# Two graph layers, fused: the hand-made order of VectorE, ScalarE and GpSimd is dropped, that of TensorE and the transfers is kept

## The chip, the cores and the metric

One NeuronCore of one Trainium2 chip runs the whole program. The metric is the device time of one execution in microseconds. For the kernel before it is 2702.02 us, the median of three runs (2701.94 to 2702.38).

## What is computed

The input `x` is 128 graphs of 128 nodes with 256 features, and `adj` is a 128x128 adjacency matrix of 0 and 1 for each graph. Everything is float32. Two layers follow each other:

```python
# layer 0: two graph attentions, then a feed-forward of 1024 with Relu
h = gat(x, W1, a1); h = gat(h, W2, a2)     # softmax over axis 1 of leaky_relu(Wh1 + Wh2^T), masked by adj
h = layernorm(x + h); x = layernorm(h + relu(h @ w_ff1) @ w_ff2)
# layer 1: 8 heads of 32, values by relation (adj == r), then a feed-forward of 1024 with Gelu
attn = softmax(q k^T / sqrt(32)); out = sum_r (attn * (adj == r)) @ v_r
x = layernorm(x + out @ Wo); x = layernorm(x + gelu(x @ W1) @ W2)
```

## The kernel before

**Tiling.** Four graphs make a group (`G = 4`), so there are 32 groups. A group passes through five stages: `load`, `gat` (both graph attentions and the first normalisation), `ff0` (Relu feed-forward), `att` (heads) and `ff1` (Gelu feed-forward). Several groups are in flight at once, each in another stage. A first part of the program, `graph_layers` (L1073), does the graph attentions of groups 0 to 2 and `ff0` of group 0, prepares the weights, and scans the whole adjacency for values other than 0 and 1; a branch (L1157) then takes one of two versions of the rest. With these inputs it is always `BINARY`; the other, `GENERAL`, is compiled but not run.

**Each stage is a generator.** It issues some instructions and then yields a number. `run` (L958) pops the stage with the smallest time from a heap, lets it issue its next piece, and pushes it back at its time plus the step. So a timetable (`begin`, `steps`, `early`, `period=100` units for one group) decides the order in which all pieces are traced. One group took about 80 us on the chip, so a unit is some 0.8 us.

**From the timetable to queues.** After each piece `run` looks at the instructions just traced. Those of TensorE and SyncE (`kept`, which issues all transfers) enter their engine's queue at the piece's time. Those of the other three engines enter their engine's queue at the piece's time plus a number from the table `lags`, where such a number is given:

```python
        for i in reversed(new):
            lag = 0 if i.engine in kept else None
            if behind.get(i.engine):
                lag = behind[i.engine].pop(0) if len(behind[i.engine]) > 1 else behind[i.engine][0]
            if lag is not None:
                queues.setdefault(i.engine, []).append((round(t + lag, 3), len(queues.get(i.engine, ())), i))
            elif lags is not None and PE in queues:
                after(i, queues[PE][-1][2])
...
    for queue in queues.values():
        queue.sort(key=lambda x: x[:2])
        for (_, _, first), (_, _, i) in zip(queue, queue[1:]):
            after(i, first)
```

Every queue is sorted by time, and each instruction is tied behind the one before it. `after` adds an ordering edge for the compiler's scheduler (`NoSync`: it fixes the order of issue and adds no semaphore). An instruction without a lag is tied only behind the last TensorE instruction that was traced before it. Among what such edges leave open the compiler chooses, with its own simulated run of the program (`schedule_with_timeline_sim=True`, L1207).

**The lag tables.** A table has one line for each piece of a stage. In it `V`, `S` and `G` are VectorE, ScalarE and GpSimd, and the numbers are lags in timetable units for that engine's instructions in that piece, the last number serving for all that follow. `BINARY` has tables for `gat`, `ff0`, `att`, `ff1`, and separate ones for some stages of the first and the last group (L77 to L251). `PREFIX`, the first part's plan, has its own (L280 to L354). `lag_table` (L996) reads them. Most numbers of `BINARY` lie near 100; only differences between them matter, since each engine has its own queue. Some stand out: the first four VectorE statistics of `att`'s last piece have 45.9 to 59.3, the affine of `att`'s second half has 9 and 14.1 on GpSimd.

**The pieces that the prediction speaks of.**
- `feed_forward` (L641) does its products by a scheme with fewer multiplications. `unit` (L651) makes one half of the hidden features in four visits; two units are interleaved by `order=(0, 0, 1, 0, 1, 0, 1, 1)`. Each visit is two `product` calls (L656, matmuls at L658) into two PSUM tiles, `chain` and `side`. Between visits the other engines read partial sums out of the same tiles, and only then may TensorE go on into them: L664 (ScalarE copies `chain`) and L665 (VectorE adds `side`) after the first visit, L669 and L670 (ScalarE copies both) after the second, L674 and L675 (VectorE adds both) after the third, and the activations L679 and L683 (ScalarE) after the fourth. The second product is at L714, and its results are added into `y` by VectorE at L719.
- `normalised` (L571) is statistics on VectorE (L577, L578, L580), a power on GpSimd (L582), one VectorE product (L583) and four scalings on ScalarE (L585). `affine` (L587, L591) is two GpSimd instructions for each two graphs.
- `put` (L593) turns a tile: VectorE transposes 32x32 blocks (L608), SyncE stores it to DRAM (L611), and `get` (L615) reads it back (L617).
- `attention` (L818): query and key (L828 to L834), scores (L849), maxima on VectorE (L853), exponentials on ScalarE (L862), division on GpSimd (L865), turning, the mask on VectorE (L884), the values (L899, L900), the weighted sum (L913), its copy (L917) and the output product (L940, L941).
- `gat_block` (L786): features (L794, copied at L795), scores and softmax (L769 to L783), and weighted sums (L802, copied at L803, and L813).

Of the kernel before, what the change touches and what calls it, by code (L numbers as in the profile page):

```python
# [25 lines left out]
G = 4  # L26
# [19 lines left out]
    lags={},  # L46
# [10 lines left out]
        gat=(  # L57
            3.6, 5.8, 1.7, 17.4, 23.25, 4.55, 12.25, 11.5, 16.85,
        ),
        ff0=(  # L60
            1.45, 19.1, 6.85, 4.85, 5.95, 3.1, 5.95, 0.1, 0.3, 0.5, 0.6, 0.4, 0.3, 0.25, 17.5, 0.2,
            0.3,
        ),
# [10 lines left out]
        (-2, "ff1"): -2, (-1, "load"): -2, (-1, "ff1"): -5, (3, "load"): 24, (-4, "load"): -10,  # L74
        (4, "load"): -7, (5, "load"): -1, (-5, "load"): -6,
    },
    lags={  # L77
        "gat": """
V 15.2 | S 104.7 95
S 102.8 104.1  # L80
V 99.9
|
V 102.7 104.7 105.4 117.1 | S 110.4 110.8 110.6 106 112.8 113.3 111.3 112.7 | G 113.4
S 97.7 98.3 99.6 100.4
V 96.7
|
V 84.8 85.6 88.4 99.3 | S 84.3 87.2 88.1 86.4 96.8 90.8 90.2 98.2 | G 102.7
V 91.7 93 92.1 92.3 93.3 95.1 96.7 97.9 98 98.2 98.4 98.6 | S 102.1 99.8 99.4 97 | G 100.7
""",
        "ff0": """  # L90
V 95.8
|
G 92.7 103.2 97.6 110.4
V 107.9 | S 107.3
S 104.3 104.8
V 102.9 | S 103.6 | G 54.9 67.7
V 103.6 104.5
S 98.8 100.9 | G 48.3 50.9
S 103.9 99.6 100.9 105 102.3 98.5
V 101.1 103.3  # L100
S 104.4 106.1 105.3 105.9 106.7 104.2
|
V 101.6 104.3 | G 106.4 100.5
V 105.4 107 | G 110.3
V 105.3 108.1 108.5 | G 104.5
V 96.3 97.5
V 100.9
V 104.4 105.5 100.6 101.4 101.5 106 106.2 107 106.6 107.1 107.3 108.7 | S 111.8 112.5 114.6 110.7 | G 107.2
""",
        "att": """  # L110
V 100.7
|
V 106.7 105 | S 102.9 114
V 103.9 106.2 107.4 108.2 110.6 117.5 | S 110.9 112.3 112.9 114.7 113.6 116 115.6 116.9 116.9 121.2 117.3 119.6 120.1 120.9 119.5 120.3 | G 110.5 119.3
V 96.6 103
|
V 110.5 112 | G 55.4 67
V 122.1 129.6
V 105.4 105.6 107.4 107.6 111.5 115.5 | S 104.5 107 108.4 107.3 108.7 108.8 109.6 109 109.9 110.5 114.3 113.2 113.6 110.2 112 113.5 115.4 | G 111.2 116.4
V 97  # L120
V 92.1 95.8
|
V 96.8 98.8 | G 9 14.1
V 106.8 108.6
S 119.4
V 105.5
V 45.9 54.2 50.8 59.3 99.3 99.9 99.7 100 100.5 102.8 | S 103.8 104 105.6 104.7 | G 97.4
""",
        "ff1": """
V 87.7  # L130
|
G 96.4 96.4 111.7 103.9
V 94.9 | S 93.9
S 100.6 92.2
V 92.8 | S 93.3 | G 48.2 62.3
V 96.3 103
S 93.3 93.9 | G 43.6 51.8
S 101.5 102.2 96.5 102.9 90.8 104.9
V 98.6 101.8
S 102.4 102.7 102 102.9 99.4 101.4  # L140
|
V 100 107 | G 92.1 106.8
V 99.7 111.4 | G 101
V 94.7 96 99.5 | G 92.2
V 97.3 100.3
V 101.3
V 65.3 67.6 64.2 64.3 66.8 68.5 70.1 72.5 70.2 72.4 74.1 75.6 | S 77.5 80.2 78.3 76.4 | G 70.5
G 34.5 80.5
G 45.7 46.4
""",  # L150
        "ff0 -1": """
V 100.1 | S 97.2
|
G 71.5 75.6 91.9 103.7
V 109.3 | S 106.9
S 104.2 106.8
V 102.4 | S 101.1 | G 68 76.2
V 105.3 101.8
S 95.4 97.11 | G 59 72.5
S 96.8 99 101.8 104.5 101.3 96  # L160
V 100.8 102.3
S 107.5 110.3 110 110.3 104.5 105.8
|
V 99.5 101.1 | G 102 107.7
V 104.2 109.7 | G 112.9
V 109.6 110.6 113.1 | G 107
V 100.1 101.3
V 101.17
V 103.9 105.7 100.99 102.2 102.1 102.6 105.9 107.2 106.1 106.48 107.8 111 | S 105.12 106.3 106.55 106.8 | G 111
""",  # L170
        "att 0": """
V 119.5 111.85 113.2 113.3 114.4 120.5 116.2 114.8 103.4 109.5 120.6 128.2 107.7 119 112.8 | S 142.2
|
V 105.3 103.7 | S 125.3 129.53
V 105.7 111.1 113 113.3 116.2 119.6 | S 125.46 125.69 125.91 126.9 126.6 126.6 126.82 127.28 127.05 129 127.2 128.2 127.5 128.9 128.64 128.87 | G 109.3 111.2
V 102.2 109.9 | S 110.35 118.1
|
V 103 112.3 | G 66.7 80.2
V 101.7 115
V 102.6 105.9 106.2 107.57 109.2 120.2 | S 98.4 101.2 103 100.3 100.9 102.6 106.3 104.6 111.7 104.4 107 113.3 114 107.7 114.3 115.1 116.9 | G 105.5 121.2  # L180
V 95.8
V 97.05 108.1 | S 102.7 120.3
|
V 104.6 115 | G 12.3 13.3
V 99.4 100
S 112
V 101.3
V 43.7 48 44.1 52.4 95.45 96.2 95.8 97.5 98.61 104.5 | S 105 109.5 109.2 108.7 | G 97
""",
        "att -1": """  # L190
V 101.6 | S 108.7
|
V 106.8 95.7 | S 101.3 101.8
V 103.2 105.6 106 106.5 112 115.8 | S 98.6 102.7 101.6 103.7 104.7 107.8 105.8 110.9 107.4 111 111.5 120 113.1 116.2 112.1 113.7 | G 111 115.6
V 99.3 101.74 | S 102.6 106.2
|
V 108.3 110.8 | G 60.1 61.3
V 99.2 102.1
V 90.2 93.7 96.7 103.7 104.7 107.2 | S 84.3 90.9 95.5 90.7 93.8 102.6 104.2 94.9 98.5 104.3 107.4 97.6 105.2 104.5 110.1 106.8 111.4 | G 90.7 96.2
V 85.8  # L200
V 98 89.3 | S 90.1 93
|
V 95.3 110.7 | G 2 6.7
V 89.8 103.6
S 93.9
V 101.8
V 43.19 53 43.6 45.4 97.3 101.93 101.85 102 102.5 103.1 | S 84.8 87.7 94 104.3 | G 92.5
""",
        "ff1 0": """
V 86.9  # L210
|
G 89.9 91.7 101 107.5
V 94.2 | S 94.56
S 90.9 93.8
V 96 | S 95 | G 48.8 53.4
V 95.6 96.2
S 92.3 92.4 | G 51.8 70.9
S 96 90.2 96.2 99.3 98.6 99.8
V 97 99.3
S 100.6 94.6 96.6 107.6 97.6 102.6  # L220
|
V 97.7 106 | G 103.9 100.1
V 103.5 107.5 | G 104.6
V 94 94.8 98.6 | G 94.1
V 96.2 97.2
V 100.1
V 66.5 68 67.5 70 67.8 71.2 70.8 71.4 71.72 72 73.9 76.4 | S 77.48 75.9 78.2 91.5 | G 70
G 39.2 54.7
G 38.6 59.9
""",  # L230
        "ff1 -1": """
V 83 | S 82.9
|
G 64.85 66.7 68.1 68
V 57.9 | S 65.5
S 62.5 62.1
V 48.2 | S 57.5 | G 40.1 53.8
V 48.8 54
S 68.4 77 | G 44.4 56.4
S 61.7 69 76.2 84.3 53.5 56.1  # L240
V 50.8 53.65
S 82.5 85.1 81.8 86.4 82.1 77.2
|
V 44.6 46.9 | G 61 83.5
V 52.7 53.4 | G 83.6
V 33.7 37.4 40.5 | G 64.3
V 37.4 41.6
V 40.6
V 4.1 9.9 7.3 9.6 10.8 15.3 13.43 15.1 18.9 20.3 20.1 23.4 25.6 28.1 27.3 28.4 32.8 32.9 | S 28.5 26.1 31.7 40.8 | G 33.8 58.3
""",  # L250
    },  # L251
)

PREFIX = dict(
# [22 lines left out]
        34, 39.75, 6.05, 33.25, 5.05, 21.05, 9.55, 19.25, 27.55, 11.55, 13.25, 8.55, 3.55, 1.55,  # L277
        4.05, 65.25, 46.05,
    ),
    lags={  # L280
        (0, 0): """
V 2 | S 16.4 3
S 9.2 4.3
|
V -15.1 -13.2 -1.6 -1.2 -0.7 -0.6 1.2 2.6 | S -4.6 -4.6 -4.6 -3.5 -1.9 -1.5 0 -1.5 | G 3 6.9
S -13.8 -11.9 -11.6 -10.3
|
V -14.6 -13.7 -12.8 -12.7 -12.4 -9.6 -9.7 -8.2 | S -22.4 -18.4 -16.6 -15.6 -13.4 -12.4 -9.4 -9.5 | G -22.2 -20.9
V -6.8 -5.6 -4.9 -3.6 -4 -3.2 -2.6 -1.8 -2.2 -1.8 -1.4 0.8 | S 0.5 0.6 3.2 3.3 | G -4.5
""",  # L290
        (0, 1): """
V 17.1 | S 14.6 16.2
S 11.3 12.6
|
V -7 -3.6 0.1 1.5 4.6 5.5 8 9 | S -9 -8 -7.5 -7 -0.2 -2.2 6.8 5.2 | G 11.3 13.8
S -20.8 -19.7 -20.6 -18.7
|
V -61.8 -60.3 -60 -59.7 -59.1 -58.1 -53.9 -46.9 | S -64.8 -64.3 -64.3 -62.8 -56.9 -55 -56.7 -53.6 | G -48.1 -42.3
V -84.5 -84.3 -83 -82.6 -83 -80.8 -81.2 -79.4 -79.3 -78.9 -75.9 -65.9 | S -66.6 -82.5 -61.4 -79.8 | G -75
""",  # L300
        (0, 2): """
V 15.7 | S 4.4 -1
S 3 6.1
|
V -9.2 -8.5 -7 -8 -6.6 -6.3 -3.8 -2.2 | S -13.6 -12.1 -11.5 -10.3 -7.9 -7 -1.8 -6.3 | G -10.5 -1.1
S -19.8 -19.5 -18.7 -18.3
|
V -52.3 -47.6 -46.8 -47.9 -47.2 -46.9 -44 -40.5 | S -57 -53.7 -53.7 -52.7 -44.2 -43.7 -42.8 -44.8 | G -52.7 -46.2
V -55.8 -53 -52.8 -52 -52.4 -50.2 -51.1 -50.8 -50.7 -49.5 -49.2 -44.6 | S -50.3 -33.2 -37.1 -41.5 | G -56.3
""",  # L310
        (1, 0): """
V -11.8 | S -11.8
|
G -35.3 -34.3 -33.4 -32.6
V -35.2 | S -36.1
S -45.8 -44.8
V -42.6 | S -44.7 | G -56.2 -55.6
V -55.4 -54
S -55 -54.5 | G -69.2 -57.6
S -57.4 -58.1 -56.2 -50.1 -55.1 -57.6  # L320
V -75 -73.7
S -87.6 -85.9 -84.1 -83.2 -85.1 -85.1
|
V -119.7 -116.8 | G -126.8 -118.6
V -136.2 -134.6 | G -132.5
V -135.8 -135.7 -135 | G -134.7
V -155.9 -155.1
V -157.4
V -194.8 -191.1 -196.4 -194.2 -195.5 -191 -190.4 -189.1 -189.5 -189 -180.8 -180.6 | S -192.8 -195.1 -193 -182.4 | G -198.9
""",  # L330
        (2, 0): """
V 11.9 13.1 11 13.3 14.7 19.9 15.7 18.2 18.9 19 24.5 21.7
V -53.6 -43.2 -42 -24.2 -47.9 -40.1 -32.2 -32.5 -40
""",
        (3, 0): """
|
V -34.5
S -44
V -69.8
S -77.1  # L340
V -83.5
S -105.3
V -123.1
S -130.4
V -149.7
S -155.3
V -151.6
S -157.7
V -156.4
S -164  # L350
V -212.8
S -264.5
""",
    },  # L354
)

_COLS = {
    "bf1": "L0_gnn_b_ff1", "b1": "L1_gnn_b1", "bq": "L1_gnn_bq", "bk": "L1_gnn_bk",
# [852 lines left out]
```

## Time and profile before

| | |
|---|---|
| median of three runs | 2702.02 us |
| the profiled execution's own time | 2707.46 us |
| its span, first to last instruction | 2705.6 us |
| mean granted TensorE clock | 0.985 |
| busy share of the span | TensorE 98%, VectorE 77%, ScalarE 61%, GpSimd 62% |
| SyncE-issued transfers, share of 16 DMA engines | 52.2% |

PE is TensorE's matmuls, PEld its weight loads, DVE VectorE, ACT ScalarE, POOL GpSimd and SP SyncE. In a row of costliest groups, the text before the bar names line, engine, operation, tiles (out<-in) and shapes with the count; behind it stand the busy time, the mean duration in ns, and the engine's idle time before these instructions with what ended it. In the view of waits a row is who waited, for what, the total us, how many times and the longest. In the timeline a row is start, duration, engine, line and operation, with idle time before it in brackets. In a table of windows each row is a stretch of the span with the busy time of PE, PEld, DVE, ACT and POOL, the granted clock, the DMA share and GB/s.

### The profile page before, as it was taken

The numbers are of one execution on the slowest core, as the hardware profiler recorded it, in microseconds if no ns is written. First come the engines' busy times: TensorE is split into PE (matmuls) and PEld (weight loads), VectorE is DVE, ScalarE is ACT, GpSimd is POOL, SyncE is SP. The second block draws the span as 40 slices with busy tenths as digits, with TensorE's granted clock in tenths as the row PEclk, the third lists the DMA queues.
The fourth block names the chain that finished last, engine by engine and source line by source line (L and its number), as shares of the span: only waits on it lengthen the run. The fifth ranks groups of instructions, "written<-read, shape, count | busy, mean of one in ns | idle before, by whom it ended". The sixth has DMA issues, their size and how long they took to land.

```text
span 2705.6 us, 54054 instructions
## 1 busy us (share of the span) xinstructions
PE 2638.0 (98%) x19686; PEld 2181.8 (81%) x19686; DVE 2090.2 (77%) x3922; ACT 1638.7 (61%) x4957; POOL 1675.0 (62%) x1354
## 2 busy tenths in 40 slices
PE   7789999999999999999999999999999999999997
PEld 5668888888888888888888888888888888888767
DVE  5657887787887788888788888778788778788654
ACT  5346666656666666666666666665666665665543
POOL 2435676667566667666666666666656666766654
PEclk8899999999999999999999999999999999999999
DMA  8125555655655655655655555565554565555310
GB/s 301 33 59 133 114 112 132 139 119 130 128 106 122 149 126 118 131 116 115 140 130 119 133 117 113 133 139 118 131 127 105 125 148 126 115 123 113 77 46 24
DMA packets 1137579, 323.71 MB, mean 120 GB/s; under 512 B 886424, under 2 KB 1106072, under 8 KB 1137176
## 3 DMA queue, kind: packets, MB, share of 16 engines
q1 hardware_dynamic: 1137304, 320.17, 52.2%
q8 instruction: 157, 2.57, 0.4%
q14 instruction: 118, 0.97, 0.1%
HBM read 192.57 MB, written 127.52 MB: 118 GB/s over the span
## 4 chain that ended last, share of the span: by engine, by line
PE 93%; DVE 4%; ACT 2%; issue 1%; POOL 1%; DMA 0%; POOLq 0%; SPq 0%; ACTq 0%; DVEq 0%
PE mm L658 29%; PE mm L714 29%; PE mm L899 8%; PE mm L794 4%; PE av L913 4%; PE mm L833 4%; PE mm L828 4%; PE mm L940 4%; PE mm L849 3%; PE mm L802 2%; PE mm L813 2%; ACT e L862 1%; PE mm L602 1%; PE mm L490 0%; DVE st L577 0%
## 5 line engine op out<-in xcount | busy, mean ns | idle before, releaser
L591 POOL TENSOR_TENSOR y<-y,ln_rows 128x512 f32<-128x512 f32 x508 | 712.2, 1422 | 136.3 <-DVE T L608 118.6
L862 ACT ACTIVATE e<-mm,nm 128x128 f32<-128x128 f32 x1024 | 363.0, 379 | 117.9 <-DVE nm L853 115.1
L582 POOL TENSOR_TENSOR rstd<-rstd,mhalf 128x4 f32<-128x4 f32 x129 | 130.5, 1012 | 387.9 <-DVE rstd L580 377.8
L585 ACT ACTIVATE y<-y,nmr,rstd 128x256 f32<-128x256 f32 x512 | 272.8, 594 | 84.2 <-DVE nmr L583 83.7
L693 POOL TENSOR_TENSOR fT<-fT 128x512 f32<-128x512 f32 x128 | 187.6, 1474 | 170.1 <-DVE sum L691 170.1
L865 POOL TENSOR_TENSOR e<-e,s 128x1024 f32<-128x1024 f32 x128 | 243.0, 1899 | 64.7 <-DVE s L864 54.3
L719 DVE TENSOR_TENSOR y<-y,mm 128x256 f32<-128x256 f32 x512 | 205.5, 402 | 72.8 <-PE mm L714 72.6
L714 PEld LDWEIGHTS mm<-w,fT 128*128 128x128 f32 x2048 | 238.7, 192 | 20.6 <-issue 20.3
L714 PE MATMUL mm<-w,fT 128*128 128x128 f32 x2048 | 247.4, 277 | 0.0
L714 PE MATMUL mm<-wf,fT 128*128 128x128 f32 x2048 | 244.4, 275 | 0.6 <-DVE other L1144 0.6
L714 PEld LDWEIGHTS mm<-wf,fT 128*128 128x128 f32 x2048 | 238.8, 192 | 2.4 <-POOL fT L693 0.8
L899 PE MATMUL mm<-wv,T 128*128 128x512 f32 x512 | 232.3, 597 | 0.0
L862 ACT ACTIVATION_READ_ACCUMULATOR e<-mm,nm 128x1 f32 x1024 | 223.8, 219 | 0.0
L853 DVE TENSOR_REDUCE nm<-mm 128x4 f32<-128x512 f32 x256 | 163.5, 681 | 71.4 <-PE mm L849 71.4
L781 ACT ACTIVATE e<-e,nm 128x128 f32<-128x128 f32 x256 | 103.3, 404 | 169.8 <-DVE nm L778 169.5
L577 DVE BATCH_NORM_STATS2 st<-y 128x6 f32<-128x256 f32 x512 | 201.9, 411 | 3.4
L679 ACT ACTIVATE fT<-fT,col 128x512 f32<-128x512 f32 x256 | 181.4, 725 | 26.7 <-DVE fT L675 26.7
L664 ACT COPY fT<-mm 128x512 f32<-128x512 f32 x128 | 75.8, 592 | 190.8 <-PE mm L658 190.8
L658 PE MATMUL mm<-T,w 128*128 128x256 f32 x768 | 183.6, 382 | 0.3 <-ACT T L606 0.3
L658 PE MATMUL mm<-T,wf 128*128 128x256 f32 x768 | 182.5, 381 | 0.0
L608 DVE STREAM_TRANSPOSE e<-e 128x1024 f32<-128x1024 f32 x120 | 149.1, 1243 | 35.2 <-POOL e L865 34.1
L899 PEld LDWEIGHTS mm<-wv,T 128*128 128x128 f32 x512 | 98.0, 192 | 96.4 <-issue 93.0
(166 smaller groups left out, 6264.5 us busy)
## 6 DMA issues: line engine op xcount, KB each, us to landing
zd<-e SPq DMA_DIRECT2D x480, 128.0 KB, 3.2
eT<-zd SPq DMA_DIRECT2D x120, 512.0 KB, 5.2
zd<-T SPq DMA_DIRECT2D x364, 128.0 KB, 3.3
T<-zd SPq DMA_DIRECT2D x91, 512.0 KB, 4.2
xt<-in_xT_dram SPq DMA_DIRECT2D x32, 512.0 KB, 3.8
y<-in_x_dram SPq DMA_DIRECT2D x32, 512.0 KB, 6.4
out_dram<-y SPq DMA_DIRECT2D x31, 512.0 KB, 5.7
e<-zsd SPq DMA_DIRECT2D x58, 256.0 KB, 4.3
```

The costliest lines, as they stand in the source:

```text
L577: nc.vector.bn_stats(st, y[:, b])
L585: nc.scalar.activation(y[:, b], y[:, b], AF.Identity, bias=nmr[:, b:b + 1], scale=rstd[:, b:b + 1])
L591: engine.tensor_tensor(y[:, b:b + n], y[:, b:b + n], v[:, None, :].to_broadcast([P, n, D]), op)
L658: nc.tensor.matmul(p[:, i], win[k][:, ts(f0 + i, P)], hs[k], start=first and i == 0, stop=True, skip_group_check=True)
L679: nc.scalar.activation(lo[:, i], lo[:, i], func, bias=bin_[:, f0 + i:f0 + i + 1])
L693: nc.gpsimd.tensor_sub(a21, a11, a21)
L714: nc.tensor.matmul(p[:, j], parts[u][k][:, i, ts(j, N)], wout[k][:, 2 * u + i], start=id(bank) not in done, stop=True, skip_group_check=True)
L719: nc.vector.tensor_add(v, v, p)
L853: nc.vector.tensor_reduce(nm.rearrange("p j i -> p (j i)"), p.rearrange("p j i n -> p (j i) n"), AX.X, OP.max, negate=True)
L862: nc.scalar.activation(e[:, k], p[:, j, i], AF.Exp, bias=nms[q][:, j, i:i + 1], accum_out=s[:, k:k + 1])
L865: nc.gpsimd.tensor_mul(e, e, per_row(s, N))
L899: nc.tensor.matmul(p, hT[:, b, f], wv[:, f], start=f == 0, stop=f == DC - 1)
```

## The change

Both `lags` dictionaries become empty. Nothing else is touched: the timetable, the queues of TensorE and SyncE, the instructions themselves, the tiles and their buffers.

```diff
@@ BINARY
-    lags={
-        "gat": """
-V 15.2 | S 104.7 95
-S 102.8 104.1
...
-V 4.1 9.9 7.3 9.6 10.8 15.3 13.43 15.1 18.9 20.3 20.1 23.4 25.6 28.1 27.3 28.4 32.8 32.9 | S 28.5 26.1 31.7 40.8 | G 33.8 58.3
-""",
-    },
+    lags={},
@@ PREFIX
-    lags={
-        (0, 0): """
-V 2 | S 16.4 3
...
-V -212.8
-S -264.5
-""",
-    },
+    lags={},
```

The callers ask `plan["lags"].get(..., "")` (L1067, L1138), and `lag_table("")` gives a list with one empty entry, not `None`. So every VectorE, ScalarE and GpSimd instruction of the two plans now takes the branch `elif lags is not None and PE in queues` of `run`: it is tied behind the TensorE instruction traced last before it, and to nothing of its own engine. The order within these three engines is the compiler's.

More of the change, by code (lines that the diff above doesn't have):

```diff
@@ L76 @@
     },
-    lags={
-        "gat": """
-V 15.2 | S 104.7 95
-S 102.8 104.1
[L81 to L88, printed above, removed]
-""",
[L90 to L108, printed above, removed]
-""",
[L110 to L248, printed above, removed]
-V 4.1 9.9 7.3 9.6 10.8 15.3 13.43 15.1 18.9 20.3 20.1 23.4 25.6 28.1 27.3 28.4 32.8 32.9 | S 28.5 26.1 31.7 40.8 | G 33.8 58.3
-""",
-    },
+    lags={},
 )
@@ L279 @@
     ),
-    lags={
-        (0, 0): """
-V 2 | S 16.4 3
[L283 to L350, printed above, removed]
-V -212.8
-S -264.5
-""",
-    },
+    lags={},
 )
```

## The prediction

> **What bounds the kernel now.** I read the page's busy shares first, then a table of windows, then the waits of TensorE, then those of the engines whose order is given up, then one stretch of the timeline.
>
> ```profile
> PE 2638.0 (98%) x19686; PEld 2181.8 (81%) x19686; DVE 2090.2 (77%) x3922; ACT 1638.7 (61%) x4957; POOL 1675.0 (62%) x1354
> ...
> 0.00:95.00 95.00, 74.47 (x366) 61.53 (x366) 58.99 (x160) 49.85 (x146) 26.78 (x35) 0.87 0.58 215
> 95.00:202.92 107.92, 86.55 (x560) 63.32 (x560) 59.64 (x96) 41.44 (x149) 45.10 (x34) 0.86 0.26 57
> 202.92:2435.04 2232.12, 2230.95 (x16813) 1851.76 (x16814) 1801.85 (x3327) 1410.71 (x4265) 1451.72 (x1162) 1.00 0.57 125
> 2435.04:2705.60 270.56, 246.04 (x1950) 205.23 (x1948) 169.72 (x340) 136.65 (x399) 151.42 (x124) 0.96 0.29 65
> ```
>
> TensorE is the bound, and in the long middle it is saturated: 1.17 us without a matmul in 2232 us. All its idle time is at the ends: 95.00 - 74.47 = 20.5 us in the first part, 107.92 - 86.55 = 21.4 us while the pipeline fills, 24.5 us while it empties. So a better order can win at most these 66 us, a worse one can lose anywhere. VectorE is at 1801.85 / 2232.12 = 81% in the middle, ScalarE at 63%, GpSimd at 65%: none binds, but VectorE has little room for standing in the wrong place.
>
> The next lines, from the waits of the weight loads in 300 to 2430 us and from the waits of ScalarE, GpSimd and VectorE over the whole span, show how close the margin is and what the lag tables buy:
>
> ```profile
> PEld mm L658 <- DVE fT L674: 10.1, 26, 0.4
> PEld mm L658 <- DVE fT L665: 8.7, 26, 0.5
> ...
> ACT fT L664 <- PE mm L658: 190.8, 65, 10.5
> ...
> ACT fT L669 <- PE mm L658: 51.9, 35, 2.6
> ...
> POOL rstd L582 <- DVE rstd L580: 377.8, 126, 10.5
> ...
> DVE fT L674 <- PE mm L658: 40.8, 38, 2.8
> ```
>
> The stretch holds some 26 groups, and about once in each TensorE's weight load already waits 0.3 to 0.4 us for the VectorE additions L665 and L674: these handoffs have no slack. And the three engines often stand idle on purpose: ScalarE waits 2.9 us at a time (190.8 / 65) for the first product of a feed-forward, GpSimd 3.0 us (377.8 / 126) for the power. They are kept free so that the next urgent instruction starts at once. One place where this is visible is the timeline at 1457 us:
>
> ```profile
> 1456.58 0.65 DVE L675 TENSOR_TENSOR fT<-fT,mm 128x512 f32<-128x512 f32 x1
> ...
> 1458.17 0.69 DVE L674 TENSOR_TENSOR fT<-fT,mm 128x512 f32<-128x512 f32 x1 [0.94 <-PE mm L658]
> 1458.77 1.32 DVE L884 TENSOR_TENSOR m<-eT,am 128x1024 f32<-128x1024 f32 x1
> ...
> 1460.30 0.84 PEld L658 LDWEIGHTS mm<-t,w 128*128 128x128 f32 x4
> ```
>
> VectorE stands idle for 0.94 us, takes L674 as soon as TensorE is done, and only then the mask L884. The mask's transfers were issued at 1451.5 and 1452.5 us; the page's 5.2 us to landing puts both before 1457.8. An order that takes what is ready would start a mask at about 1457.2, perhaps both (1.32 + 1.18 us), and L674 would end near 1460.4 and not at 1458.86: the 1.4 us that TensorE had in hand (it loads these weights at 1460.30) are gone.
>
> [...] ScalarE sits 3.1 us for one copy (L670) at 1444 us. [...] the trace has 62 loads of 1283 ns[...].
>
> **The change, part by part.** No instruction, transfer or semaphore-bearing dependence is added or removed as work, so there is no new busy time. TensorE's and SyncE's orders stay.
>
> *(a) Handoffs inside the feed-forwards.* The trace has 128 units (L664 x128). TensorE depends in each on three ScalarE copies (L664, L669, L670: 384) and two VectorE additions (L665, L674: 256); L675 only frees a buffer and feeds the activation. Under the compiler's order such an instruction, which is traced last, finds what was ready before it. From the durations of all VectorE instructions in 300 to 2430 us (sum of squares over twice the sum) the rest of a running one is 0.43 us on average, the mean one 0.60 us; on ScalarE the rest is 0.25 us. I estimate for VectorE a chance of 0.6 of meeting a running one and 0.4 of one more ahead: 0.6 x 0.43 + 0.4 x 0.60 = 0.50 us. For ScalarE, 0.5 x 0.25 = 0.13 us. TensorE has other matmuls between visits (1.0 to 1.9 us, L794, L802, L813), and about half of the margins are near zero, so I let half reach it: 256 x 0.25 + 384 x 0.065 = 64 + 25 = 89 us. L664 and L665 lie ahead of the same visit, as do L669 and L670, so I take off a quarter: 67 us. Bounds: all hidden, 0; all of it reaches TensorE, 256 x 0.50 + 384 x 0.13 = 178 us. These chances are my choice; the trace of before has no such order. The cover that makes the low end possible are the matmuls between visits; where it is gone, each late handoff costs its own time.
>
> *(b) The normalisations and GpSimd.* The power L582 (1.01 us) may now stand behind up to four affines of 1.42 us (5.7 us). SyncE issued the store of a turned tile at 1419.30 us, 4.1 us after its transpose ended (1413.94 + 1.25). Mostly hidden: I take 0; what it costs when uncovered is a rival below. The four early statistics of `att` (two of 0.41 and two of 0.17 us, 1.2 us) now come after the last output product; the same 4.1 us cover them. The deferred affines become work that fills gaps: no gain, since TensorE doesn't wait for them.
>
> *(c) Activation tables.* Gelu runs from 1453.4 to 1465.3 us in the group looked at; the exponentials around it end at 1440.6 and begin at 1472.9, after scores that TensorE makes at 1471.0. TensorE's order keeps them apart, so I take 62 loads as before: 0. If one pair more came in each of 31 groups, ScalarE would have 31 x 2 x 1.28 = 80 us more work, which its 37% of free time hides unless it stands before a copy.
>
> *(d) The ends.* In the first part and the filling TensorE already waits; the scans and the statistics now fall where they are ready, but none ahead of its place among TensorE's instructions. The last group's tail is one chain. From -15 (a third of the 21.4 + 24.5 us idle in filling and emptying) to +20 us (the first part's idle time doubled); I take +8.
>
> Sum: 67 + 0 + 0 + 8 = 75 us. The profiled execution took 2707.46 us with a span of 2705.6; 1.9 us lie around it. 2707.46 + 75 = 2782. The median of the runs is 5.4 us lower, so 2702 + 75 = 2777 us.
>
> **The rivals.**
> - *The likeliest, 2777 us (2735 to 2850):* handoffs stand in line, spread thinly over all feed-forwards. Chance 0.50.
> - *Mostly covered, 2721 us (2708 to 2735):* dependences leave little choice, and a quarter of the 75 us remains (19). For it: the trace starts most instructions within about two us of their inputs. Against: the weight loads that wait already. Chance 0.20.
> - *A jam behind SyncE, 2900 us (above 2850):* the power comes 5.7 us late, 1.6 us more than the 4.1 us of cover; the store, and all transfers behind it in SyncE's fixed order, are late, and TensorE with them. Four chains in each of 31 groups at 1.6 us: 198 us. For it: GpSimd is kept idle 378 us for just this. Against: the pow's place seldom meets four affines. Chance 0.16.
> - *No difference, 2702 us:* data and the edges behind TensorE's instructions leave nearly the same order; the change then does not do what it says. Chance 0.07.
> - *Faster, 2687 us:* the middle keeps its cover, and work that no longer stands behind an idle engine shortens filling and emptying by a third of 45.9 us. It decides from the point where (a) costs under 10 us, that is under 0.08 us for each of the 128 units. For it: the engines' purposeful idling is cheap to give up where TensorE waits anyway. Against: the same tables have entries of their own for the last group. Chance 0.07.
>
> **How the numbers follow.** A measurement of this kernel can tell 0.2%, 5.4 us, from no change. Faster by over 0.2% has the last case, 0.07; within it the fourth, 0.07; slower the other three, 0.50 + 0.20 + 0.16 = 0.86. The range of 2697 to 2880 takes in no change and the upper bound of (a), 178 us; outside lie the faster case (0.07) and most of the jam (about 0.11).
>
> **What would show each step right or wrong.** TensorE's busy time in the profile after should stay near 2638 us, with the lost time as gaps in the middle stretch. (a) is right if the waits of TensorE and its weight loads for L664, L665, L669, L670 and L674 grow from some 30 us over the whole span (13.6 + 11.0 + 3.7 + 1.4 + 0.5) to over 80, with ScalarE's idle 190.8 us before L664 shrunk; wrong if the gaps are at L714, L849, L913 or L940. (b) shows in SyncE's own waits for L608 and in TensorE waiting for GpSimd's L635 to L638. (c) is wrong with far more than 62 table loads. (d) shows in the first two windows. The prediction falls if the middle has no gaps at all, or if gaps of several us recur once a group at one place.

## The result and the profile after

The kernel after takes 3230.78 us, the median of four runs (3228.24 to 3231.26), against 2702.2 us (2701.94 to 2706.2) for the kernel before on the same chip. The ratio is 1.194 (95% interval 1.193 to 1.196). The direction was forecast; the size was not: 75 us were forecast, 529 came, and the time lies far outside the range.

In this profile line numbers are 248 lower than in the kernel before, because the tables are gone: L410 is its L658 (products of the feed-forward), L416 and L417 its L664 and L665, L421 and L422 its L669 and L670, L426 its L674, L466 and L471 its L714 and L719, L535 its L783, L636 its L884, L334, L335 and L337 its L582, L583 and L585 (the normalisation's power, product and scalings), L565 its L813. The kernels of the experiments keep the numbers of the kernel before.

The page's busy shares:

```profile
PE 2807.9 (87%) x19686; PEld 2241.0 (69%) x19686; DVE 2033.6 (63%) x3922; ACT 1629.6 (50%) x4957; POOL 1682.4 (52%) x1354
```

The same instructions, 19686 matmuls among them, but TensorE is busy for 87% of the span, not 98%, and its busy time is 170 us longer. The mean granted clock is 0.947, where it was 0.985. The windows (length, then busy time of TensorE, its weight loads, VectorE, ScalarE and GpSimd, the clock, the DMA share and GB/s), the first two cut as they were for before:

```profile
0.00:95.00 95.00, 72.61 (x366) 59.98 (x366) 59.16 (x160) 51.63 (x148) 27.86 (x35) 0.93 0.60 215
95.00:203.00 108.00, 79.45 (x536) 58.27 (x536) 48.47 (x81) 36.00 (x129) 31.63 (x25) 0.82 0.22 53
203.00:2930.00 2727.00, 2404.73 (x16969) 1918.72 (x16970) 1756.09 (x3343) 1410.49 (x4313) 1465.39 (x1168) 0.96 0.47 103
2930.00:3230.00 300.00, 251.14 (x1818) 204.04 (x1816) 169.85 (x338) 131.50 (x373) 157.56 (x127) 0.91 0.25 58
```

The first part idles 22.4 us, as before (20.5). The middle, which had 1.2 us without a matmul, now has 2727.00 - 2404.73 = 322 us.

The bill can be closed from the trace. All gaps of over 50 ns between matmuls sum to 407.1 us, where they were 53.8: 353 us more. TensorE's busy time grew by 169.9 us. Together 523 us, and the span grew by 523.8. Stretches in which the trace's clock record is 0.5 (half speed below) explain a good half of the busy growth, by an estimate from the trace: they cover 347.1 us, where they covered 83.2. In the kernel after the matmuls L410 from `T` with `wf` start every 427 ns within them (median) and every 216 ns outside. TensorE was busy in 251 us of them (60 before) and stood idle in the rest, so half of the difference, 96 us, is put down to the slow clock; it would be 132 us had TensorE been busy throughout. The other 74 us of busy time were not attributed.

Where the gaps are, by the waits of TensorE (waiter, what it waited for, total us, times, longest):

```profile
PE mm L410 <- DVE fT L417: 133.2, 60, 4.3
PE mm L466 <- DVE y L471: 84.2, 41, 2.4
PE mm L410 <- ACT fT L416: 35.8, 29, 1.4
PE mm L410 <- DVE fT L426: 34.0, 30, 3.1
PE mm L565 <- POOL e L535: 29.7, 31, 4.1
```

There are 32 groups, so each row is one place, or two, that recurs in every group. The feed-forward places L416, L417 and L426 were expected; L535 was not, and a gap at L466, the old L714, had been named as a sign that (a) is wrong. The waits that answer to those shown of before, of the weight loads, ScalarE, GpSimd and VectorE:

```profile
PEld mm L410 <- DVE fT L417: 158.0, 62, 4.7
...
PEld mm L410 <- DVE fT L426: 59.4, 64, 3.5
...
ACT fT L416 <- PE mm L410: 108.2, 79, 5.5
ACT fT L421 <- PE mm L410: 94.3, 34, 5.7
...
ACT y L337 <- DVE nmr L335: 304.6, 85, 12.5
...
POOL rstd L334 <- DVE rstd L332: 319.9, 122, 9.3
...
DVE m L636 <- DMA eT<-zd: 246.1, 116, 5.3
...
DVE fT L426 <- ACT fT L435: 156.7, 34, 4.9
```

The weight loads' 11.0 and 13.6 us over the span for L665 and L674 have become 158 and 59 us. VectorE itself now stands at the head of its queue: 246 us with the mask product L636, because the turned tile has not landed (before, L884 had 6 us of idle time ahead of it in all), and 157 us with L426, because of an activation (33 us before). ScalarE stands 305 us with the scaling L337, because the normalisation's product is late; in the kernel before this row was

```profile
ACT y L585 <- DVE nmr L583: 83.7, 69, 14.3
```

One such place in the timeline (start, duration, engine, line, operation, idle time before it):

```profile
1285.10 2.87 SPq L369 DMA_DIRECT2D eT<-zd  x2
...
1286.50 0.60 ACT L337 ACTIVATE y<-y,nmr,rstd 128x256 f32<-128x256 f32 x1 [5.68 <-DVE nmr L335]
...
1287.00 0.57 ACT L416 COPY fT<-mm 128x512 f32<-128x512 f32 x1
...
1287.71 1.10 PE L410 MATMUL mm<-t,wf1s 128*128 128x256 f32 x4 [1.37 <-ACT fT L416]
...
1290.15 1.28 DVE L636 TENSOR_TENSOR m<-eT,am 128x1024 f32<-128x1024 f32 x1 [3.69 <-DMA eT<-zd]
1291.36 0.67 DVE L417 TENSOR_TENSOR fT<-fT,mm 128x512 f32<-128x512 f32 x1
...
1292.09 2.07 PE L410 MATMUL mm<-t,wf1s 128*128 128x256 f32 x4 [3.27 <-DVE fT L417]
```

The addition L417 could have run from 1287.57, when the copy L416 ended. But the mask is ahead of it and waits for a transfer that was issued at 1285.10; VectorE does nothing for 3.69 us, then the mask takes 1.28, then comes the addition, and TensorE has lost 3.27 us. The instruction ahead is not a running one, as the prediction had it, but a waiting one. A little earlier the same happened on ScalarE: the scaling L337 stood 5.68 us for its normalisation, the copy L416 came behind it, and TensorE lost 1.37 us.

### The profile page after: what moved, and what is told of

The parts are those of the page before. It is cut to its first block, busy times and chain, and to the rows that moved or that the text cites. A ratio compares the mean times of both kernels' runs of the same rounds, so it can differ in the third digit from the quotient of the medians.

```text
span 3229.4 us, 53861 instructions
## 1 busy us (share of the span) xinstructions
PE 2807.9 (87%) x19686; PEld 2241.0 (69%) x19686; DVE 2033.6 (63%) x3922; ACT 1629.6 (50%) x4957; POOL 1682.4 (52%) x1354
## 4 chain that ended last, share of the span: by engine, by line
PE 45%; DVE 14%; ACT 14%; DMA 11%; issue 11%; POOL 4%; SPq 1%; DVEq 0%; POOLq 0%; ACTq 0%
PE mm L410 19%; DMA eT<-zd 9%; ACT e L614 7%; PE mm L466 7%; PE mm L580 4%; PE mm L651 4%; PE mm L585 3%; DVE e L528 2%; PE mm L565 2%; PE mm L554 2%; PE mm L692 2%; ACT e L521 1%; DVE e L529 1%; ACT y L337 1%; DVE e L360 1%
## 5 line engine op out<-in xcount | busy, mean ns | idle before, releaser
L343 POOL TENSOR_TENSOR y<-y,ln_rows 128x512 f32<-128x512 f32 x508 | 667.0, 1321 | 19.4
L445 POOL TENSOR_TENSOR fT<-fT 128x512 f32<-128x512 f32 x128 | 205.7, 1607 | 843.8 <-DVE sum L443 745.5
L337 ACT ACTIVATE y<-y,nmr,rstd 128x256 f32<-128x256 f32 x512 | 271.2, 612 | 304.7 <-DVE nmr L335 304.6
L636 DVE TENSOR_TENSOR m<-eT,am 128x1024 f32<-128x1024 f32 x128 | 166.6, 1303 | 246.3 <-DMA eT<-zd 246.1
L466 PE MATMUL mm<-w,fT 128*128 128x128 f32 x2048 | 259.7, 281 | 67.0 <-DVE y L471 66.0
L466 PEld LDWEIGHTS mm<-w,fT 128*128 128x128 f32 x2048 | 244.5, 194 | 93.1 <-DVE y L471 71.3
L334 POOL TENSOR_TENSOR rstd<-rstd,mhalf 128x4 f32<-128x4 f32 x129 | 131.2, 1017 | 339.9 <-DVE rstd L332 319.9
L410 PE MATMUL mm<-t,wf1s 128*128 128x256 f32 x512 | 158.6, 450 | 136.1 <-DVE fT L417 96.8
L466 PE MATMUL mm<-wf,fT 128*128 128x128 f32 x2048 | 249.6, 277 | 17.7 <-DVE y L471 16.0
L466 PEld LDWEIGHTS mm<-wf,fT 128*128 128x128 f32 x2048 | 239.6, 192 | 26.3 <-POOL rstd L334 16.9
L614 ACT ACTIVATION_READ_ACCUMULATOR e<-mm,nm 128x1 f32 x1024 | 248.1, 242 | 0.0
L410 PEld LDWEIGHTS mm<-t,wf1s 128*128 128x128 f32 x512 | 105.8, 218 | 174.3 <-DVE fT L417 109.5
L410 PE MATMUL mm<-T,wf 128*128 128x256 f32 x768 | 223.5, 443 | 0.1
L471 DVE TENSOR_TENSOR y<-y,mm 128x256 f32<-128x256 f32 x512 | 193.3, 402 | 38.1 <-PE mm L466 33.8
L410 PEld LDWEIGHTS mm<-T,wf 128*128 128x128 f32 x768 | 175.6, 232 | 55.1 <-issue 14.8
L410 PE MATMUL mm<-T,w 128*128 128x256 f32 x768 | 186.8, 387 | 4.4 <-DMA T<-zd 3.6
```

What stands on the lines that cost most here:

```text
L337: nc.scalar.activation(y[:, b], y[:, b], AF.Identity, bias=nmr[:, b:b + 1], scale=rstd[:, b:b + 1])
L343: engine.tensor_tensor(y[:, b:b + n], y[:, b:b + n], v[:, None, :].to_broadcast([P, n, D]), op)
L410: nc.tensor.matmul(p[:, i], win[k][:, ts(f0 + i, P)], hs[k], start=first and i == 0, stop=True, skip_group_check=True)
L445: nc.gpsimd.tensor_sub(a21, a11, a21)
L466: nc.tensor.matmul(p[:, j], parts[u][k][:, i, ts(j, N)], wout[k][:, 2 * u + i], start=id(bank) not in done, stop=True, skip_group_check=True)
L471: nc.vector.tensor_add(v, v, p)
```

## The experiments

All times are single runs beside a run of the kernel before (2707.0, 2703.0, 2707.9, 2701.9 and 2707.7 us for the five sets in order), so a few us mean nothing. "Over before" is against that run.

**Theory 1: the waiting mask products carry the loss.** Rivals: short queues of runnable work, as in the prediction; a jam behind SyncE; a plan whose parts rely on one another, so that no place alone carries it. The first run moves the masks later in the kernel after, the second moves them early in the kernel before.

*e1, masks later in the kernel after* (two steps of `att` 10 units longer, the following ones as much shorter; the orders of TensorE and SyncE stay):

```diff
-            2.8, 17.5, 4.45, 19.45, 0.15, 0.55, 0.35, 31.6, 22.6, 0.3, 0.45, 2.45, 5.7, 22.3, 14.15,
+            2.8, 17.5, 4.45, 19.45, 0.15, 0.55, 10.35, 21.6, 22.6, 0.3, 0.45, 2.45, 15.7, 12.3, 14.15,
```

> The kernel after, with one thing moved: in the timetable of att the piece that issues the mask products (L884) comes 10 units, some 8 us, later in both halves, and the step behind it is 10 units shorter, so that the orders of TensorE and SyncE stay as they are. Theory 1 (VectorE stands at a mask whose turned tile has not landed, and the feed-forward additions behind it are late): VectorE's wait at L884, 246 us after, falls below 60; TensorE's waits for L665 and L674, 167 us after, fall by more than half; the clock rises from 0.947; time 2950 to 3090. Theory 2 (many short queues, no single place): L884 stops waiting but TensorE's waits stay, time 3180 to 3240.

Measured 3164.4 us, 66 less than after, between the two expectations. The masks' wait fell from 246 to 40 us and TensorE's for L665 from 133 to 57, but those for L719 grew from 84 to 112 and for L783 from 30 to 60. Theory 1 expected twice to four times as much; the loss moved on.

*e2, masks early in the kernel before:*

```diff
-V 122.1 129.6
+V 112.1 112.2
...
-V 106.8 108.6
+V 98.8 98.9
```

> The kernel before, with only the VectorE lags of the two mask pieces in att lowered by 8 to 17 units, so that both masks of a half stand where the kernel after has them, ahead of the feed-forward additions. Nothing else moves. Theory 1: VectorE waits 2 to 4 us at the first of each pair for its transfer, twice in a group, and TensorE loses 3 to 5 us in each of some 30 groups, more with the clock: 2800 to 2900. Theory 2: the masks are 2.4 us of work at another place, TensorE loses less than 1 us in a group: 2700 to 2735.

Measured 3119.2 us, 412 over before, from the places of four instructions of each group in `att`. Both expectations were too low. *e5* makes only the second of the two edits, *e12* makes it about half as large (`V 102.8 104.6`), so that both products stand ahead of just one pair of additions, L675 and L674:

> The kernel before with one line of the tables changed: of each half's second mask step in the last third of att, the two mask products (L884) are ordered some 8 to 10 us earlier on VectorE; the other mask pair stays late. Both pairs early gave 3119 us, 412 us over before. If each misplaced pair costs on its own (an early product waits for its own transfer and holds up whatever stands behind it): the half of that, 150 to 260 us, so 2855 to 2965 us, with L884 waiting for its transfer about 60 times. If it takes both (VectorE runs out of slack only with four early products): below 60 us, 2702 to 2765. If one of the two places carries nearly all: either below 2740 or above 3060.

> The kernel before with one line of the tables 4 us earlier: of the second mask step's two products both now stand just ahead of the additions L675 and L674 in VectorE's order, in place of one after them and one after the transpose L608; nothing else moves. Eight us earlier cost 241 us (2944), with one gap of some 4.4 us in each group. If the product's wait for its transfer and its 1.3 us of work add up in front of L674: L674 comes 2.5 us of work and 1 to 2 us of wait later, minus 1.4 us in hand, a gap of 2 to 3 us in each of 29 groups and a half clock stretch each: 60 to 90 us plus 50 to 70: 2810 to 2870 us. If the distance doesn't matter, only that it is ahead: 2920 to 2960. If these two additions have slack after all: below 2740.

e5 measured 2944.2 us (241 over before, within the first expectation, that each pair costs on its own; the other pair was not moved alone), e12 2765.6 us (58 over, below the expectation). The row of TensorE's waits for the addition, first in e12, then in e5:

```profile
PE mm L658 <- DVE fT L674: 48.0, 29, 3.5
```

```profile
PE mm L658 <- DVE fT L674: 127.2, 29, 6.0
```

One gap in each group, of 48.0 / 29 = 1.7 us in the one and 4.4 us in the other. The difference in cost is larger than that of the gaps: in e12 all gaps grew by 46 us, the half-speed stretches from 83 to 87 us, that is hardly at all, and TensorE's busy time by 12; in e5 the gaps grew by 147 us and the stretches to 278 us, and TensorE's busy time by 89. e12 missed its range because its gaps were shorter than the 2 to 3 us expected, and because it counted a slow stretch for each.

*e6* has the early places of e2, but the product's input is on the chip already:

```diff
-nc.vector.tensor_tensor(m, eT, at[:, b][:, None, :].to_broadcast([P, H, N]), OP.mult)
+nc.vector.tensor_tensor(m, hT.rearrange("p b c n -> p (b c) n"), at[:, b][:, None, :].to_broadcast([P, H, N]), OP.mult)
```

> As the run with both mask pairs early (3119 us), but the product reads the group's hidden state hT, which has been on the chip for long, in place of the turned tile eT: same shape, type, engine and place, so the same work at the same early place, without the wait for the transfer. (The output is not the reference's.) If the loss comes from standing in line behind an instruction that waits for its transfer: it is gone, 2700 to 2745 us. If it comes from 1.3 us of work standing ahead of the additions (short queues, as the prediction had it): each of some 120 products delays at most one addition by 1.3 us, half of them reach TensorE, 80 us and some clock on top: 2780 to 2900 us. If it comes from the other instructions that move with it: above 3000 us.

Measured 2826.1 us, 123 over before: 289 of e2's 412 us go with the wait, and what is left lies in the range of the rival, work that stands ahead. Its path is not the one that I had thought of, as the timeline shows:

```profile
1339.90 2.35 DVE L884 TENSOR_TENSOR m<-T,am 128x1024 f32<-128x1024 f32 x2
...
1343.50 0.17 DVE L580 TENSOR_SCALAR rstd<-mv 128x4 f32<-128x4 f32 x1
1343.74 1.01 POOL L582 TENSOR_TENSOR rstd<-rstd,mhalf 128x4 f32<-128x4 f32 x1 [5.87 <-DVE rstd L580]
...
1344.79 1.22 DVE L583 SCALAR_TENSOR_TENSOR nmr<-mv,rstd 128x4 f32<-128x4 f32 x1 [1.12 <-POOL rstd L582]
...
1346.04 0.60 ACT L585 ACTIVATE y<-y,nmr,rstd 128x256 f32<-128x256 f32 x1 [2.18 <-DVE nmr L583]
1346.54 0.56 ACT L670 COPY fT<-mm 128x512 f32<-128x512 f32 x1
...
1347.16 1.26 PE L658 MATMUL mm<-T,w1s 128*128 128x256 f32 x4 [1.95 <-ACT fT L670]
```

What the masks hold up here is not an addition that TensorE stands for, but the statistics behind them (L580). So the power on GpSimd is late, so the scaling L585, at the head of ScalarE's queue, waits 2.18 us, and the copy L670 behind it comes late for TensorE. A delay on VectorE has become one on ScalarE, by way of GpSimd (5.87, 1.12 and 2.18 us of idle time at L582, L583 and L585), and then 1.95 us without a matmul.

*e11* makes e6's edit in the kernel after:

> The kernel after, but the mask product reads the hidden state hT, long on the chip, in place of the turned tile eT, so that it never waits for a transfer (the output is not the reference's; TensorE's order is the same, VectorE's moves a little because the masks are ready sooner). In the kernel after the mask products stood 246 us before a transfer, and TensorE waited 133 + 34 us for the additions behind them, each gap of some 3 us with half a clock stretch of 3.4 to 6.8 us. If these waits carry their own share of the loss: 150 to 300 us less than 3231, so 2930 to 3080. If the places limit one another, so that removing one uncovers the next: above 3130. If the masks carry everything: below 2800.

Measured 3255.1 us, 24 more than after, as the second expectation had it, although no mask waits for a transfer any more. TensorE's waits are now

```profile
PE mm L813 <- POOL e L783: 112.1, 30, 6.0
PE mm L714 <- DVE y L719: 90.0, 46, 3.6
PE mm L658 <- DVE fT L665: 65.0, 40, 3.4
PE mm L658 <- ACT fT L669: 46.1, 31, 3.8
```

The wait for L665 halved, the one for L783 went from 30 to 112 us. So early masks are enough for a loss (e2), but not what the loss of the kernel after needs. Theory 1 fell here.

**Theory 2: the tables are one plan, and its parts are worth something only together.** First by engine. These kernels keep the first part's tables; in the second part they keep only the engines that the last column of the diff names, and tie nothing behind TensorE's instructions:

```diff
-            elif lags is not None and PE in queues:
+            elif False:
...
-def lag_table(text):
+def lag_table(text, kept):
...
-... for q in line.split("|") if q.strip()}
+... for q in line.split("|") if q.strip() and q.split()[0] in kept}
...
+... lag_table(..., "VS")    # e7; "VG" in e9, "SG" in e10, "V" in e4, "-" in e3
```

> The second part has no tables, as after, and in addition its VectorE, ScalarE and GpSimd instructions are no longer tied behind TensorE's; the first part keeps its tables. The compiler is wholly free in these three engines. Theory 1: the masks are placed by the same simulated landing, so about as after, 3130 to 3280. Rival (the ties behind TensorE's instructions are what costs, by holding work back): well below, under 3000.

> As the run before this one, but VectorE keeps its tables in the second part; ScalarE and GpSimd are in the compiler's order. Theory 1 (VectorE's order carries the loss): at least three quarters of the loss is gone, 2710 to 2830. Rival (GpSimd's and ScalarE's order carry it, since GpSimd stood idle 745 us for L693 after): 2950 or more.

> Second part: VectorE and ScalarE keep their tables, GpSimd alone goes by the compiler's order, nothing tied behind TensorE's instructions. If the tables are a joint plan in which every engine's order relies on the others' (VectorE alone kept: 3149 us, 446 over): GpSimd feeds the power, two of the twelve mask and sum steps and the deferred affines, on which TensorE and VectorE wait less often than on ScalarE's copies; 2760 to 2960 us, with GpSimd's late results (L582, L691, L783) as the largest waits. If only VectorE's and ScalarE's orders matter: 2702 to 2730. If GpSimd's order is the one that carries the loss: above 3050.

> Second part: VectorE and GpSimd keep their tables, ScalarE alone goes by the compiler's order, nothing tied behind TensorE's instructions. GpSimd alone free cost 40 us (2743), ScalarE and GpSimd free together 446 (3149). If the loss of that pair is ScalarE's, because VectorE's kept order waits for ScalarE's copies and exponentials in turn: 3050 to 3170 us. If it takes both engines together: below 2850. If free engines are slow only because their order differs from the fixed ones' in either direction, any one engine would do, but GpSimd's 40 us already speaks against that.

> Second part: ScalarE and GpSimd keep their tables, VectorE alone goes by the compiler's order, nothing tied behind TensorE's instructions. VectorE is the busiest of the three and its order holds the early mask products: 3000 to 3350 us if its order is the main carrier, with L884 waiting for its transfers again and TensorE waiting for L665, L674 and L719. If the ScalarE order is the main carrier and VectorE's only follows: 2750 to 2900 us.

| free in the second part | time, us | over before |
|---|---|---|
| GpSimd (e7) | 2742.7 | 40 |
| ScalarE (e9) | 3196.0 | 488 |
| VectorE (e10) | 3226.1 | 518 |
| ScalarE and GpSimd (e4) | 3148.6 | 442 |
| all three, untied (e3) | 3445.1 | 738 |
| all three, tied (the kernel after) | 3230.8 | 529 |

e7 came between its first two expectations, e4 fell to the rival, e9 came just above its first one, e10 within it, and e3 above all: the ties behind TensorE's instructions help by 214 us, and I had not expected that they do. All rows but the last are without these ties, so they are to be held against the 738 us of e3: ScalarE's order alone or VectorE's alone costs two thirds of it, GpSimd's alone a twentieth. What one engine costs with the ties kept was not run. How one engine does it is plain in e9, where VectorE still follows its planned order:

```profile
1254.02 0.34 SPq L766 DMA_DIRECT2D e<-zsd  x1
...
1257.74 1.28 ACT L769 ACTIVATE e<-e,wh 128x128 f32<-128x128 f32 x4 [6.94 <-DMA e<-zsd]
1259.04 1.28 ACT L862 ACT_TABLE_LOAD   x1
...
1265.85 0.20 DVE L864 RECIPROCAL s<-s 128x8 f32<-128x8 f32 x1 [6.78 <-ACT e L862]
...
1265.97 0.70 DVE L719 TENSOR_TENSOR y<-y,mm 128x256 f32<-128x256 f32 x2
...
1266.40 1.86 PE L714 MATMUL mm<-w2s,sum 128*128 128x128 f32 x7 [6.00 <-DVE y L719]
```

ScalarE stands 6.94 us with the graph attention's L769, whose transfer has not landed; the heads' exponentials L862, whose maxima were coming from 1254.5 us on, are behind it. VectorE comes to the reciprocal L864, at the place that the plan gave it, and stands 6.78 us for those exponentials. Behind that stands the addition L719, and TensorE loses 6.00 us. In the whole trace VectorE's wait for L862 grew from 39.4 us (36 times) to 321.5 (66 times). An engine that keeps the good order is stopped by it.

Then by part of the layer. These drop the tables of some stages for all three engines, tied as in the kernel after:

```diff
-plan["lags"].get(...)
+{q: v for q, v in plan["lags"].items() if not q.startswith(("ff0", "ff1"))}.get(...)    # e13; ("att",) in e14, ("gat",) in e15, both in e16
```

> The tables of both feed-forwards dropped (copies, additions, activations, sums and normalisations in the compiler's order, tied behind TensorE's instructions), those of attention and graph attention kept, so no mask product and no softmax moves against its like. The prediction's step (a), with the additions and copies waiting behind whatever is running: 2770 to 2880 us. If the loss needs the attention's early instructions standing ahead of them: below 2740. If any stage out of the plan loses all (as one engine out of plan did): above 3100.

> The tables of the attention (att, and its variants for the first and last group) dropped, the three others kept, tied as in the kernel after. If early attention instructions (mask products, exponentials, reciprocals) standing ahead of the fixed additions carry the loss: 2950 to 3200 us. If it takes several stages out of plan together: 2750 to 2900. If the feed-forwards' own order carries it: below 2750.

> The tables of the graph attention (gat) dropped, the others kept. In the kernel after its two softmax steps (4.3 us of VectorE beside GpSimd) stood ahead of the addition L719 and cost TensorE 2.4 us once a group. If such a place costs on its own: 2770 to 2900 us. If the plan of the others leaves slack for it: below 2740. If any stage out of the plan loses all: above 3100.

> Attention and graph attention free, both feed-forwards on their tables. If what stands ahead is attention's and graph attention's and the feed-forwards are only its victims: as slow as the kernel after, 3100 to 3300 us. If the feed-forwards' own order carries half: 2850 to 3050.

| free stages | time, us | over before |
|---|---|---|
| `gat` (e15) | 2891.1 | 189 |
| both feed-forwards (e13) | 3203.0 | 501 |
| `att` (e14) | 3369.6 | 668 |
| `att` and `gat` (e16) | 3237.7 | 536 |
| all four (the kernel after) | 3230.8 | 529 |

Nothing adds up: 501 + 668 + 189 is 1358, and `att` alone free is worse by 139 us than everything free. A part in its planned order among parts that aren't can be no help. But not every part is needed by the others: with `gat` alone free, or GpSimd alone, most of the plan's worth stays (189 and 40 us lost). e13 came where its third expectation had it, e15 and e16 within their first, e14 above all three. e13 is the nearest to step (a) alone. There TensorE waits for the feed-forwards' own L664, L665, L670 and L674 only 26.2 + 5.0 + 8.6 + 59.6 = 99 us; the bulk is another row:

```profile
PE mm L714 <- DVE y L719: 281.7, 62, 8.8
```

and the timeline of one of these waits goes through four queues:

```profile
1189.63 3.48 SPq L611 DMA_DIRECT2D zd<-T  x4
...
1193.22 0.54 SPq L766 DMA_DIRECT2D e<-zsd  x1
...
1197.19 1.28 ACT L769 ACTIVATE e<-e,wh 128x128 f32<-128x128 f32 x4 [11.13 <-DMA e<-zsd]
...
1198.50 0.69 DVE L776 SCALAR_TENSOR_TENSOR e<-e 128x512 f32<-128x512 f32 x1 [6.20 <-ACT e L769]
...
1203.55 0.41 DVE L719 TENSOR_TENSOR y<-y,mm 128x256 f32<-128x256 f32 x1
...
1204.10 1.20 PE L714 MATMUL mm<-wf,fT 128*128 128x128 f32 x4 [7.64 <-DVE y L719]
```

The turned tile's store (L611) held SyncE until 1193.1 and the graph attention's load behind it came late; ScalarE stood 11.13 us for it, VectorE 6.20 us for ScalarE, and the addition L719, a few instructions further back in VectorE's queue, made TensorE wait 7.64 us.

**The rivals about places.** *e8* empties the first part's tables alone, *e17* takes SyncE out of the kept orders of the kernel after (`run(tc, todo, (PE,))` at both callers), *e18* keeps none (`run(tc, todo, ())`):

> Tables kept in the second part, dropped in the first (encoder, filters, filling of the pipeline; three engines tied behind TensorE's instructions as in the kernel after). The kernel after loses its time once in every group, so the first part should carry little: 2702 to 2735 us (the prediction took 8 us for all ends, at most 20 for this part). If the first part's order throws the second part's fixed plan out of step: above 2800.

> The kernel after, with SyncE's transfers in the compiler's own order as well; TensorE alone follows the timetable. If the loss is a jam behind SyncE's fixed order (the prediction's rival): most of the 524 us come back, below 2900 us. If late results of VectorE and ScalarE make the transfers late, whatever their order: within 100 us of the kernel after, 3130 to 3330.

> All five orders the compiler's own, no timetable. If a fixed TensorE order is what the free engines can't follow: better than the kernel after by over 150 us, below 3080. If orders from a simulated run are late by the same kind of waits on every queue, TensorE's included: 3100 to 3600 us. Below 2702 is not expected by either: TensorE's busy time alone is 2638 us.

e8 measured 2707.6 us, 4.5 over before: the first part carries nothing that can be told from no change. e17 measured 3269.1 us, 38 above after: giving up SyncE's fixed order doesn't help, so it is not what jams; transfers that are late in either order are not excluded. e18 measured 3339.0 us, 108 above after, but it changes one thing more: where TensorE has no fixed queue, `run` ties nothing behind its instructions. e3 lacks these ties too and keeps the orders of TensorE and SyncE (and the first part's tables), and it took 3445.1 us, 106 more than e18. So e18 doesn't show that TensorE's fixed order helps the others: without the ties, the kernel with the fixed orders is the slower one, and with them TensorE was never freed. None of the eighteen beats the kernel before.

## Why the prediction was wrong

**What failed is step (a), the size of a handoff.** The place was right for the larger part: TensorE's own waits for L664, L665, L670 and L674 (now L416, L417, L422, L426) sum to 35.8 + 133.2 + 10.5 + 34.0 = 213.5 us, where 67 were forecast, and ScalarE's idle time before L664 shrank from 190.8 to 108.2 us. But even the upper bound, 178 us, was below that. It took what stands ahead of an addition to be running or runnable work, and a late addition to cost 0.50 us. That half of the handoffs reach TensorE was about right for L665 (60 of 128); the size was not: the measured wait is 133.2 / 60 = 2.2 us. Followed back one by one in the trace, 30 of these waits (97 us, 3.2 us each) and 29 of the 30 for L674 have a mask just ahead that stands for its transfer. Ahead of 28 others for L665 nothing waits (35 us, 1.25 us each): work in line, as predicted, but more than twice as much of it. And all 29 waits for the copy L664 (35.8 us) have a scaling L585 just ahead that stands for its normalisation. A sum over instruction durations can't see the waits. e6 and e2 part the two sizes for the mask: 123 us with the input landed, 412 without.

**The places were not all there.** L719 and L783 (84.2 + 29.7 = 114 us) had no term, and gaps at L714, where TensorE waits for L719, were the prediction's own sign that (a) is wrong. In 28 of the 41 waits for L719, VectorE had just stood with the graph attention's L776 for ScalarE's L769. The prediction took the handoffs of different engines as independent and let each cost its own time; e6, e9 and e13 show one delay pass through three or four queues before it reaches TensorE.

**"No new busy time" was wrong.** It held for work and not for time: 170 us more, of which the slow clock makes about 96 by the estimate above. The signpost "TensorE busy should stay near 2638" is refuted. This term is a third of the whole loss and had no place in the sum at all.

**(b), the normalisations and GpSimd, at 0** was too low. GpSimd's order alone costs 40 us (e7). Late normalisations cost more than that: ScalarE stands 304.6 us for them (83.7 before), and the 35.8 us for L664 lie behind such waits. The sign named for (b), SyncE's own waits for L608's turned tile, grew from 101.7 to 293.7 us. This is a way that the prediction had seen, the power late, but the damage came through ScalarE's queue and not only through the store. Its rival, the jam behind SyncE at 2900 us, is not shown as the cause: freeing SyncE's order brought nothing (e17), and e6 and e13 show the power and the transfers as links of longer chains.

**(c), the activation tables, at 0:** the trace after has 31 + 30 + 1 = 62 loads of 1283 ns, as forecast. **(d), the ends, at +8:** the first part measured +4.5 us in e8. In the windows, TensorE idles 28.6 us while the pipeline fills and 48.9 us while it empties, 31.5 us more than before and above the +20 allowed. How much of that is the loss of every group, running into the ends, was not measured.

The prediction was to fall if "gaps of several us recur once a group at one place". Such gaps came: 30 of 3.2 us each before L665. At the other places gaps recur as well, but are smaller, 1.0 to 2.1 us on average.

**What stays open.** That the compiler put the masks too early because the transfers land earlier in its simulated run than on the chip (5.2 us for `eT<-zd` there, by the page) was my guess; no run shows it. Which chain fixes the 16 us (524 / 32) that the kernel after loses in each group is not settled: every place that was relieved (e1, e11) uncovered another, so there may be no single one. Why `att` free is slower than all free is not known. Nor is what TensorE's fixed order does for the others, since no run frees it with the ties kept. The clock's share was read from the traces and not varied by itself.

## What to carry to other kernels

When an order is given up on engines where one waiting instruction holds those behind it, as on ScalarE (6.94 us) and VectorE (6.78 us) in e9, don't price an instruction that comes late by what runs ahead of it, but by the longest wait that may stand ahead of it, and follow that wait through the next queue. An order that has been planned across engines can be worth little in parts: here the feed-forwards or `att` alone out of plan cost about as much as all stages or more (501 and 668 us against 529), `gat` alone 189. If TensorE is the bound, add to gaps of 2 us and more the slow clock, which followed 427 of 465 such gaps here where they stood alone (counted below).

## What the runs showed of the hardware

**Half speed after gaps of TensorE.** Over the traces of all twenty kernels I took the gaps of TensorE in the middle (from 230 us after the start to 300 us before the end) that had no other gap of over 0.3 us within 10 us on either side, and counted those with half speed right after. Of gaps of 0.3 to 1.5 us 3 of 309 were followed by it, of 1.5 to 2 us 24 of 124, of 2 to 3 us 116 of 148, of 3 to 3.5 us 42 of 47, of 3.5 us and more 269 of 270. In the kernel after alone it was none of 16 of 0.3 to 2 us and 9 of 9 of 2 to 3 us; longer lone gaps do not occur there. All but one of the 752 half-speed stretches in the middle of the twenty traces last 3.4, 6.8 or 10.2 us; in the kernel after 23 last 3.4 us and 22 last 6.8 us.

**VectorE beside GpSimd.** The product L777 (128x512, two operands in SBUF) takes 0.68 us in the kernel before where no GpSimd instruction runs beside it (28 cases, median) and 1.42 us where one, L693, runs throughout (29 cases). In the kernel after none of the 58 runs alone: 29 fall beside the division L865 (median 2.27 us), 29 partly beside an affine (1.44 us). The maximum L853 and the addition L665, which read PSUM, take about the same either way in the kernel before: L853 0.68 us, L665 0.67 us alone and 0.69 us beside GpSimd.
